# The 64-row parts of q, k and v of a token tile side by side, in the input products of a transformer block

## The chip, the core and the metric

The kernel runs on one core of a Trainium2 chip. A core has a matrix engine (TensorE, "PE" in the profile; "PEld" is its loading of the stationary operand), three elementwise engines (VectorE "DVE", ScalarE "ACT", GpSimd "POOL"), an engine that mostly issues transfers (SyncE "SP"), and DMA engines. Each engine works through its own list of instructions in order; semaphores tie the lists together. The metric is the device time of one execution in microseconds (us), the median of three runs.

## The reference

One block of a diffusion transformer over x of 2 batches x 2048 tokens x 576 features, 16 heads of 36, in float32:

```python
xn = _ln(x, 1e-06) * (1 + sc_msa) + sh_msa            # modulated from cond
qkv = (xn @ w_qkv + b_qkv).reshape(B, N, 3, H, hd)    # 576 -> 1728
q, k, v = qkv[:, :, 0], qkv[:, :, 1], qkv[:, :, 2]
q = _ln(q, 1e-05, qn_g, qn_b)                         # per head
k = _ln(k, 1e-05, kn_g, kn_b)
attn = softmax(einsum('bqhd,bkhd->bhqk', q, k) * hd ** (-0.5))
o = einsum('bhqk,bkhd->bqhd', attn, v).reshape(B, N, C)
x = x + g_msa * (o @ w_proj + b_proj)
xn2 = _ln(x, 1e-06) * (1 + sc_mlp) + sh_mlp
x = x + g_mlp * (gelu(xn2 @ w1 + b1) @ w2 + b2)
```

## The kernel before

The work goes in stages: a short preparation of the conditioning, then for each batch the input stage (norm, q/k/v products), attention, and the output product; then the two products of the MLP for both batches. The change touches the input stage only, which is the function `inputs` (line 868).

**Tiling of the input products.** A batch is 16 token tiles of 128 tokens. The 576 features are the contracted dimension: four full chunks of 128 and one of 64. A product (q, k or v of one token tile) has two halves of 288 columns, which lie in two banks of one PSUM tile. Each half needs four matmuls over 128 rows (`whole`, line 376, matmuls on line 379) and one over 64 rows (`halved`, line 387, matmuls on line 390). The two 64-row matmuls of a product use the upper and the lower half of TensorE's rows: half 0 reads rows 0 to 63, half 1 rows 64 to 127 of a chunk that is stored twice. Going from 128-row to 64-row matmuls changes how TensorE's array is divided into tiles.

`two_products` (line 394) orders the two parts of a product by a running number 3t + w: even ones do `whole` then `halved`, odd ones `halved` then `whole`. So the 64-row parts of two products in a row lie side by side, four matmuls in a group, and there are 24 such groups in the 48 products of a batch.

**What else happens in a token tile.** Around the products stand, for each tile t:
- `next_rows` (941): the rows of tile t+2 are loaded and normed on VectorE (lines 272 to 279), with a root and a copy on ScalarE;
- `input_by_feature` (851): the normed rows of tile t+1 are transposed on TensorE (lines 357, 358) into a PSUM tile, and five ScalarE activations (line 365) apply the modulation and write `xnt`, the stationary operand of the next tile's products;
- bias additions on VectorE, which empty the PSUM tile of a product: line 960 for q and k into `both`, line 967 for v into the value tile `vt`;
- `centred` (877): head means of `both` are taken off on VectorE (lines 883 to 885), and ScalarE squares the rest (890);
- `head_scale` (892) for tile t-1: sums of squares (895), a root on ScalarE (901), a reciprocal (903), and the product on GpSimd (905);
- `by_feature` (910) for tile t-2: nine transposes of q and k on TensorE (915) into two PSUM tiles, which VectorE (924) and ScalarE (920) empty with gain and bias. At some tiles it also prepares keys or queries for attention on VectorE (lines 792, 793) whose DMAs were issued a call before.

**What sets the order.** TensorE's list follows the program's text throughout, VectorE's follows it within `inputs`; the lists of ScalarE, GpSimd and SyncE are ordered by a scheduler. PSUM tiles of this stage come from a pool of four (two banks each, `s_tile`, line 86); a fifth waits for the oldest to be emptied. Attention that follows takes all eight banks singly (`bank`). The last tile of a batch centres q and k one by one and does its own `head_scale` at once, so that attention can transpose the last two tiles between its first scores (`last`, line 935). Attention's first steps are `scores` (line 1012), exponentials on ScalarE (line 1016), and `values` (line 1025).

Of the kernel before, what the change touches and what calls it, by code (L numbers as in the profile page):

```python
# [12 lines left out]
ALU = mybir.AluOpType  # L13
# [9 lines left out]
FULL = 4  # L23
# [8 lines left out]
def dit_block(  # L32
# [25 lines left out]
    nc = tc.nc  # L58
    B, N, C = x.shape
    MLP = w1.shape[1]  # L60
    HD = qn_g.shape[0]
    H = C // HD
    NT = N // P
    NPAIR = H // 2
    HALF = C // 2
# [20 lines left out]
    def s_tile():  # L86
        return psum["s"].tile([P, 2, 512], F32, tag="s", name="s")
# [35 lines left out]
    def halves(ap):  # L123
        return ap.rearrange("p (a f) -> p a f", a=2)
# [15 lines left out]
    with tc.tile_pool(name="bound", bufs=1, side="right") as bound:  # L140
# [11 lines left out]
        product = bound.tile([1, 1], F32, name="product")  # L152
# [223 lines left out]
    def whole(outs, stationary, moving, first):  # L376
        for a in range(2):
            for k in range(FULL):
                nc.tensor.matmul(  # L379
                    outs[a],  # L380
                    stationary(k, a),
                    moving(k, a),
                    start=(first and k == 0),
                    stop=(not first and k == FULL - 1),
                )

    def halved(outs, stationary, moving, first):
        for a in range(2):
            r = slice(64 * a, 64 * a + 64)
            nc.tensor.matmul(  # L390
                outs[a], stationary(FULL, a)[r], moving(FULL, a)[r], start=first, stop=not first
            )

    def two_products(outs, stationary, moving, turn):


        parts = (whole, halved) if turn % 2 == 0 else (halved, whole)
        for part in parts:
            part(outs, stationary, moving, part is parts[0])
# [325 lines left out]
    def block_of_small():  # L725
# [16 lines left out]
        vv = vt[:, 0 : NT * H * HV].rearrange("p (t h e) -> p t h e", t=NT, h=H)  # L742
# [108 lines left out]
        def input_by_feature(b, rows):  # L851
            xnt = xs["pool"].tile([P, NKC, P], F32, name="xnt", bufs=2)
            modulated(xnt, rows, 0, b)
            return xnt
# [13 lines left out]
        def inputs(b, weights, work, xnt, loaded):  # L868

            wq, wq4, bq = weights  # L870
            normed, squares, taken = {}, {}, []
            key_tiles = (0, 4, 8, 12, 14, 16)

            def banks_of_two():
                return [bank for ps in (s_tile(), s_tile()) for bank in (ps[:, 0], ps[:, 1])]

            def centred(both, w0=0, w1=2):

                part = both[:, w0 * C : w1 * C]
                heads = part.rearrange("p (h d) -> p h d", d=HD)  # L880
                n = (w1 - w0) * H
                sums = work.tile([P, 2 * H], F32, name="sums", bufs=2)
                nc.vector.tensor_reduce(sums[:, :n], heads, AX.X, ALU.add)
                nc.vector.tensor_scalar_mul(sums[:, :n], sums[:, :n], 1.0 / HD)
                nc.vector.tensor_tensor(
                    heads, heads, sums[:, :n].unsqueeze(2).to_broadcast([P, n, HD]), ALU.subtract
                )
                if w0 == 0:
                    squares["sq"] = work.tile([P, 2 * C], F32, name="sq")
                nc.scalar.activation(squares["sq"][:, w0 * C : w1 * C], part, AF.Square)  # L890

            def head_scale(t, both, parts=((0, 2),)):
                var = work.tile([P, 2 * H], F32, name="var")
                for w0, w1 in parts:
                    nc.vector.tensor_reduce(
                        var[:, w0 * H : w1 * H],
                        squares["sq"][:, w0 * C : w1 * C].rearrange("p (h d) -> p h d", d=HD),
                        AX.X,
                        ALU.add,
                    )  # L900
                nc.scalar.activation(var, var, AF.Sqrt, bias=eps5, scale=1.0 / HD)
                inv = work.tile([P, 2 * H], F32, name="inv")
                nc.vector.reciprocal(inv, var)
                heads = both.rearrange("p (h d) -> p h d", d=HD)
                nc.gpsimd.tensor_tensor(
                    heads, heads, inv.unsqueeze(2).to_broadcast([P, 2 * H, HD]), ALU.mult
                )
                normed[t] = both

            def by_feature(t, banks, chunks=range(NQK), all_on_vector=False):  # L910
                both, begun = normed[t], [*taken]
                taken.clear()
                parts = [(c, banks[i // 4][:, i % 4 * P : i % 4 * P + P]) for i, c in enumerate(chunks)]
                for c, ps in parts:
                    nc.tensor.transpose(ps, both[:, c * P : (c + 1) * P], ident)  # L915

                for c, ps in parts[::-1]:
                    dst = chunk(c, slice(t * P, (t + 1) * P))
                    if c < 4 and not all_on_vector:
                        nc.scalar.activation(  # L920
                            dst, ps, AF.Identity, bias=bias_qk[:, c : c + 1], scale=gain_qk[:, c : c + 1]
                        )
                    else:
                        nc.vector.tensor_scalar(
                            dst, ps, gain_qk[:, c : c + 1], bias_qk[:, c : c + 1], ALU.mult, ALU.add
                        )
                for do in begun:
                    do()
                if t == TPB - 1:
                    taken.append(take_q(0, 0))  # L930
                if t + 1 in key_tiles and NQK - 1 in chunks:
                    i = key_tiles.index(t + 1)
                    taken.append(take_k_block(*key_tiles[i - 1 : i + 1]))

            def last(t, chunks):
                by_feature(t, [bank() for _ in range(0, len(chunks), 4)], chunks, True)
                left = [*taken]
                taken.clear()
                return left

            def next_rows(t):
                return tile_normed(loaded.pop(0)) if loaded else input_rows(b, t, nc.sync)

            rows = next_rows(1)
            before = None
            for t in range(NT):
                both = work.tile([P, 2 * C], F32, name="both", bufs=3)
                for w in range(3):
                    ps = s_tile()
                    two_products(  # L950
                        [ps[:, a, :HALF] for a in range(2)],
                        lambda k, a: xnt[:, k, :],
                        lambda k, a: (
                            wq[:, k, w * C + a * HALF : w * C + (a + 1) * HALF] if k < FULL else wq4[:, w, :]
                        ),
                        3 * t + w,
                    )
                    bias = halves(bq[:, w * C : (w + 1) * C])
                    if w < 2:
                        nc.vector.tensor_tensor(  # L960
                            halves(both[:, w * C : (w + 1) * C]), ps[:, :, :HALF], bias, ALU.add
                        )
                        if w == 0 and t > 0:
                            head_scale(t - 1, before)
                    else:
                        heads = "p a (h d) -> p a h d"
                        nc.vector.tensor_tensor(
                            vv[:, t, :, 0:HD].rearrange("p (a h) d -> p a h d", a=2),
                            ps[:, :, :HALF].rearrange(heads, d=HD),
                            bias.rearrange(heads, d=HD),  # L970
                            ALU.add,
                        )

                    if w == (1 if t % 2 == 0 else 0):
                        if t + 1 < NT:
                            ahead = input_by_feature(b, rows)
                        if t >= 2:
                            by_feature(t - 2, banks_of_two())
                        if t + 2 < NT:
                            rows = next_rows(t + 2)  # L980

                    if t == NT - 1 and w < 2:
                        centred(both, w, w + 1)
                    if t == NT - 1 and w == 1:
                        head_scale(t, both, ((0, 1), (1, 2)))
                if t + 1 < NT:
                    centred(both)
                before, xnt = both, ahead

            return last  # L990
# [624 lines left out]
```

## Time and profile before

| | |
|---|---|
| three runs | 3227.92, 3229.68, 3230.13 us; median 3229.68 |
| profiled execution | 3230.55 us, of it a span of 3228.7 us |
| TensorE busy | 3205.6 us (99% of the span) |
| VectorE, ScalarE, GpSimd busy | 1451.2, 1496.8, 355.1 us |
| input stage of the second batch (from 1118.0 to 1359.3 us) | TensorE 241.3, VectorE 158.3, ScalarE 79.3, GpSimd 32.4 us busy |
| share of the chain that ended last: line 379, line 390 | 16%, 2% |

The span is the profiled part from the first to the last instruction of the core; the execution's own time is a little longer. A line of a group names the source line, the engine, the operation, what is written and what is read, the shapes, how often, then busy time in us, the mean duration of one in ns, and the engine's idle time before them with what ended it. Each float32 matmul shows as two records of TensorE. Records of matmuls overlap, since they are pipelined, so distances between starts are the better measure of TensorE's time. Line 379 serves the input products and the output product, which the names of the tiles tell apart (`wq,xnt` and `wp,qo`). A line of the timeline gives start, duration and what ran, with consecutive equal instructions merged.

### The profile page before, as it was taken

Reading aid. Unit: us, or ns where it says so; the run is one execution under the profiler, and the core shown is the slowest. Engines: PE = TensorE matmul, PEld = TensorE weight load, DVE = VectorE, ACT = ScalarE, POOL = GpSimd, SP = SyncE. Lnnn points to the kernel's source line nnn. Section 1 sums busy time; section 2 is a strip of 40 time slices with the busy share of each in tenths; the row PEclk is TensorE's granted clock in tenths of the full one; section 3 lists DMA queues with packets and bytes.
Section 4 is the critical chain, followed back from the end, with each engine's and each line's share of the span. In section 5 each row is a group of like instructions: output and inputs, shape, how many; then the busy total and the mean of one; then the engine's idle time right before and its main releaser. Section 6 shows DMA issues by size and latency. Waiting matters only on the chain.

```text
span 3228.7 us, 46968 instructions
## 1 busy us (share of the span) xinstructions
PE 3205.6 (99%) x18143; PEld 1883.0 (58%) x18143; DVE 1451.2 (45%) x2131; ACT 1496.8 (46%) x2952; POOL 355.1 (11%) x432
## 2 busy tenths in 40 slices
PE   8999999999999999999999999999999999999999
PEld 5775333333333777733333333358888888777777
DVE  4674333333333366633333333345555544455454
ACT  2335666666666033366666666633555552000000
POOL 1111000112110111100001111010000000111111
PEclk9999999999999999999999999999999999999999
DMA  3112212223231400122222223154322223433331
GB/s 131 26 26 65 76 35 68 66 70 83 69 85 34 146 26 24 27 56 46 50 44 65 68 66 74 47 173 156 120 90 88 93 80 110 153 132 111 118 103 38
DMA packets 129332, 253.16 MB, mean 78 GB/s; under 512 B 22979, under 2 KB 68492, under 8 KB 127052
## 3 DMA queue, kind: packets, MB, share of 16 engines
q1 hardware_dynamic: 105588, 182.07, 18.5%
q0 software_dynamic: 22640, 66.23, 7.4%
q8 instruction: 145, 2.38, 0.3%
q10 hardware_dynamic: 872, 1.77, 0.2%
q14 instruction: 87, 0.71, 0.1%
HBM read 135.40 MB, written 66.35 MB: 62 GB/s over the span
## 4 chain that ended last, share of the span: by engine, by line
PE 99%; DMA 1%; SPq 0%; DVE 0%; issue 0%; DVEq 0%
PE b L1025 28%; PE b L1012 19%; PE s L379 16%; PE s L1527 15%; PE m L1368 12%; PE s L390 2%; PE m L1382 2%; PE one L1368 2%; PE s L915 1%; PE s L357 1%; PE t L1428 0%; DMA wq<-in_w_qkv_dram 0%; DMA wa<-in_w_ada_dram 0%; PE b L192 0%; PE b L915 0%; DMA km<-qo 0%
## 5 line engine op out<-in xcount | busy, mean ns | idle before, releaser
L1016 ACT ACTIVATE pt<-b 128x512 f32<-128x512 f32 x2048 | 1057.4, 608 | 485.6 <-PE b L1025 270.8
L1025 PE MATMUL b<-pt,vt 128*64 128x512 f32 x4096 | 935.0, 598 | 0.0
L1025 PEld LDWEIGHTS b<-pt,vt 128*64 128x64 f32 x4096 | 271.9, 136 | 582.0 <-issue 438.8
L1012 PE MATMUL b<-qm,km 32*128 32x512 f32 x4096 | 566.5, 614 | 0.2 <-DMA km<-qo 0.2
L1073 DVE TENSOR_TENSOR ot<-b,ot 128x512 f32<-128x512 f32 x192 | 132.8, 691 | 653.2 <-PE b L1025 652.7
L1012 PE MATMUL b<-qe,ke 16*128 16x512 f32 x2048 | 422.8, 790 | 0.0
L379 PE MATMUL s<-wq,xnt 128*128 128x288 f32 x1536 | 392.9, 411 | 3.9 <-DMA wq<-in_w_qkv_dram 3.2
L1527 PE MATMUL s<-ws,as 128*128 128x288 f32 x1440 | 351.8, 406 | 0.0
L1012 PEld LDWEIGHTS b<-qm,km 32*128 32x128 f32 x4096 | 191.6, 184 | 269.3 <-ACT pt L1016 205.0
L379 PEld LDWEIGHTS s<-wq,xnt 128*128 128x128 f32 x1536 | 286.4, 191 | 95.5 <-issue 18.9
L1527 PEld LDWEIGHTS s<-ws,as 128*128 128x128 f32 x1440 | 273.6, 190 | 75.6
L1044 DVE RECIPROCAL den<-den 128x512 f32<-128x512 f32 x64 | 213.6, 3337 | 12.3 <-DMA den<-den_dram 12.3
L1368 PE MATMUL m<-xnt,wb 128*128 128x256 f32 x864 | 213.8, 383 | 0.0
L1368 PE MATMUL m<-s,wb 128*128 128x256 f32 x864 | 210.1, 379 | 0.2 <-DVE s L1338 0.2
L1071 DVE COPY ot<-b 128x512 f32<-128x512 f32 x64 | 44.3, 692 | 334.7 <-PE b L1025 334.7
L1368 PEld LDWEIGHTS m<-xnt,wb 128*128 128x128 f32 x864 | 159.1, 190 | 32.2 <-issue 11.9
L1368 PEld LDWEIGHTS m<-s,wb 128*128 128x128 f32 x864 | 164.1, 190 | 22.9 <-DVE s L1338 0.6
L1012 PEld LDWEIGHTS b<-qe,ke 16*128 16x128 f32 x2048 | 108.1, 184 | 114.4 <-issue 113.0
L1395 DVE TENSOR_TENSOR cs<-m,cs 128x512 f32<-128x512 f32 x72 | 49.7, 690 | 213.1 <-ACT cs L1394 151.7
L1527 PE MATMUL s<-ws,hidden 128*128 128x288 f32 x576 | 142.3, 406 | 0.0
L1505 DVE TENSOR_TENSOR as<-hidden 128x1152 f32<-128x1152 f32 x80 | 139.0, 1801 | 0.0
L365 ACT ACTIVATE xnt<-s,mod 128x128 f32<-128x128 f32 x180 | 66.8, 460 | 152.7 <-PE s L358 152.7
(174 smaller groups left out, 2553.5 us busy)
## 6 DMA issues: line engine op xcount, KB each, us to landing
gelu<-cs SPq DMA_DIRECT2D x144, 256.0 KB
hidden<-gelu SPq DMA_DIRECT2D x16, 2304.0 KB
den<-den_dram SPq DMA_DIRECT2D x128, 128.0 KB
x_dram<-kr POOLq DMA_DIRECT2D x48, 288.0 KB, 2.8
qm<-qo SPq DMA_DIRECT2D x192, 64.0 KB
kr<-in_x_dram POOLq DMA_DIRECT2D x32, 288.0 KB, 3.8
xr<-x_dram SPq DMA_DIRECT2D x32, 288.0 KB
out_dram<-y POOLq DMA_DIRECT2D x30, 288.0 KB, 3.8
```

Of the source, the lines that this page charges most:

```text
L365: nc.scalar.activation(dst[:, k, :], t4[:, k * P : (k + 1) * P] if k < FULL else t1[:, :P], AF.Identity, bias=mod[:, which, k, b : b + 1], ...
L379: nc.tensor.matmul(outs[a], stationary(k, a), moving(k, a), start=(first and k == 0), stop=(not first and k == FULL - 1),)
L390: nc.tensor.matmul(outs[a], stationary(FULL, a)[r], moving(FULL, a)[r], start=first, stop=not first)
L1012: nc.tensor.matmul(ps, k[r, keys], q[r, :], start=first, stop=not first)
L1016: nc.scalar.activation(pt[:, h, :], banks[2 * c + h], AF.Exp, scale=SCALE)
L1025: nc.tensor.matmul(acc[64 * h : 64 * h + 64, :], vt[:, v0 : v0 + 64], pt[:, h, :], start=pt is pts[0][0], stop=pt is pts[-1][0],)
L1044: nc.vector.reciprocal(den, den)
L1073: nc.vector.tensor_tensor(ot, acc, ot, ALU.add)
L1368: nc.tensor.matmul(out_m[m], wb[:, slot[m], k, f * P : (f + 1) * P], moving[m](k), start=k == 0 and (m == 1 or (first and m in (2, 5, 6))) ...
L1382: nc.tensor.matmul(out_m[m], w[r, f * P : (f + 1) * P], a[r, FULL, t * PAIR : (t + 1) * PAIR], start=first and m != 4, stop=not first and ...
L1505: nc.vector.tensor_tensor(stationary[m], x_, y_, op)
L1527: nc.tensor.matmul(ms[m], stationary[m][:, f, :], ws[m][:, f, :], start=(f == 0), stop=(f == HF - 1))
```

## The change

The three products of a token tile are no longer made one after the other. Each gets its PSUM tile from `product`, and its two parts are issued apart: the full-row part of q, then the transposes of the next tile's rows and the norm of the rows after, the full-row part of k, then the 64-row parts of q, k and v side by side, six matmuls in one group, and then the full-row part of v. The 64-row part of v is the first of its sum, those of q and k are the last of theirs. The bias additions follow as `biased`, and `by_feature` of tile t-2 stands at the end of the tile instead of after q or k. The last tile (`final`) has no next tile: it puts the 64-row parts of q and k together, and makes v on its own at the end, with its 64-row part last; there the bias addition of v comes before the last `head_scale`.

```diff
+            def product(w, xnt):
+                ps = s_tile()
+                return ps, (
+                    [ps[:, a, :HALF] for a in range(2)],
+                    lambda k, a: xnt[:, k, :],
+                    lambda k, a: (
+                        wq[:, k, w * C + a * HALF : w * C + (a + 1) * HALF] if k < FULL else wq4[:, w, :]
+                    ),
+                )
+
+            def biased(w, ps, t, both):
+                bias = halves(bq[:, w * C : (w + 1) * C])
+                if w < 2:
+                    nc.vector.tensor_tensor(halves(both[:, w * C : (w + 1) * C]), ps[:, :, :HALF], bias, ALU.add)
+                else:
...
             for t in range(NT):
                 both = work.tile([P, 2 * C], F32, name="both", bufs=3)
-                for w in range(3):
-                    ps = s_tile()
-                    two_products(
...
-                        3 * t + w,
-                    )
...
-                        if w == 0 and t > 0:
-                            head_scale(t - 1, before)
...
-                    if w == (1 if t % 2 == 0 else 0):
-                        if t + 1 < NT:
-                            ahead = input_by_feature(b, rows)
-                        if t >= 2:
-                            by_feature(t - 2, banks_of_two())
-                        if t + 2 < NT:
-                            rows = next_rows(t + 2)
-
-                    if t == NT - 1 and w < 2:
-                        centred(both, w, w + 1)
-                    if t == NT - 1 and w == 1:
-                        head_scale(t, both, ((0, 1), (1, 2)))
-                if t + 1 < NT:
+                final = t == NT - 1
+                q, q_parts = product(0, xnt)
+                whole(*q_parts, True)
+                if not final:
+                    ahead = input_by_feature(b, rows)
+                    if t + 2 < NT:
+                        rows = next_rows(t + 2)
+                k, k_parts = product(1, xnt)
+                if not final:
+                    whole(*k_parts, True)
+                    v, v_parts = product(2, xnt)
+                halved(*q_parts, False)
+                halved(*k_parts, final)
+                if not final:
+                    halved(*v_parts, True)
+                biased(0, q, t, both)
+                if t > 0 and final:
+                    head_scale(t - 1, before)
+                if final:
+                    whole(*k_parts, False)
+                    centred(both, 0, 1)
+                    biased(1, k, t, both)
+                    by_feature(t - 2, banks_of_two())
+                    v, v_parts = product(2, xnt)
+                    whole(*v_parts, True)
+                    halved(*v_parts, False)
+                    centred(both, 1, 2)
+                    biased(2, v, t, both)
+                    head_scale(t, both, ((0, 1), (1, 2)))
+                else:
+                    biased(1, k, t, both)
+                    if t > 0:
+                        head_scale(t - 1, before)
+                    whole(*v_parts, False)
+                    biased(2, v, t, both)
+                    if t >= 2:
+                        by_feature(t - 2, banks_of_two())
                     centred(both)
                 before, xnt = both, ahead
```

More of the change, by code (lines that the diff above doesn't have):

```diff
@@ L942, in next_rows @@
                 return tile_normed(loaded.pop(0)) if loaded else input_rows(b, t, nc.sync)
+            def product(w, xnt):
[12 more added lines that the diff above has]
+                else:
+                    heads = "p a (h d) -> p a h d"
+                    nc.vector.tensor_tensor(
+                        vv[:, t, :, 0:HD].rearrange("p (a h) d -> p a h d", a=2),
+                        ps[:, :, :HALF].rearrange(heads, d=HD),
+                        bias.rearrange(heads, d=HD),
+                        ALU.add,
+                    )
             rows = next_rows(1)
@@ L947, in inputs @@
                 both = work.tile([P, 2 * C], F32, name="both", bufs=3)
-                for w in range(3):
-                    ps = s_tile()
-                    two_products(
[L951 to L955, printed above, removed]
-                        3 * t + w,
-                    )
[L958 to L962, printed above, removed]
-                        if w == 0 and t > 0:
-                            head_scale(t - 1, before)
[L965 to L972, printed above, removed]
-                    if w == (1 if t % 2 == 0 else 0):
-                        if t + 1 < NT:
-                            ahead = input_by_feature(b, rows)
-                        if t >= 2:
-                            by_feature(t - 2, banks_of_two())
-                        if t + 2 < NT:
-                            rows = next_rows(t + 2)
-                    if t == NT - 1 and w < 2:
-                        centred(both, w, w + 1)
-                    if t == NT - 1 and w == 1:
-                        head_scale(t, both, ((0, 1), (1, 2)))
```

## The prediction

> **What bounds the kernel now.** I read the page's engine shares and its chain first, then the groups of the two product lines, then the chain in order of time, and last the timeline around the end of the input stage of the second batch. The share of the chain by engine:
>
> ```profile
> PE 99%; DMA 1%; SPq 0%; DVE 0%; issue 0%; DVEq 0%
> ```
>
> TensorE is the whole chain, so only its own time counts, plus any wait that the change gives it. The groups of the two product lines (busy us, mean ns, idle before):
>
> ```profile
> L379 PE MATMUL s<-wq,xnt 128*128 128x288 f32 x1536 | 392.9, 411 | 3.9 <-DMA wq<-in_w_qkv_dram 3.2
> L390 PE MATMUL s<-wq,xnt 64*128 64x288 f32 x384 | 59.6, 429 | 0.0
> ```
>
> Each matmul of the program is two records ("passes"): 768 full-row and 192 half-row ones. They wait only at the very start. From the chain in time, 32 passes of the output stage with no 64-row part between:
>
> ```profile
> 2160.78 7.76 PE s L379 x32
> ```
>
> So a pass costs 7.76/32 = 0.2425 us. From the timeline, the last tiles of the second batch (start, duration, engine, line):
>
> ```profile
> 1343.93 1.24 PE L390 MATMUL s<-wq,xnt 64*128 64x288 f32 x8
> 1345.10 4.15 PE L379 MATMUL s<-wq,xnt 128*128 128x288 f32 x16
> ...
> 1349.09 1.15 PE L915 MATMUL s<-ident,both 128*128 128x128 f32 x9
> ...
> 1350.07 4.05 PE L379 MATMUL s<-wq,xnt 128*128 128x288 f32 x16
> ...
> 1352.03 1.27 DVE L924 TENSOR_SCALAR kr<-s,gb_qk 128x128 f32<-128x128 f32 x4
> ...
> 1353.53 0.74 DVE L883 TENSOR_REDUCE sums<-both 128x16 f32<-128x576 f32 x1
> ...
> 1354.04 1.24 PE L390 MATMUL s<-wq,xnt 64*128 64x288 f32 x8
> ...
> 1355.19 0.75 DVE L960 TENSOR_TENSOR both<-s,bq 128x576 f32<-128x576 f32 x1
> 1355.21 4.15 PE L379 MATMUL s<-wq,xnt 128*128 128x288 f32 x16
> ...
> 1357.65 1.58 DVE L895 TENSOR_REDUCE var<-sq 128x16 f32<-128x576 f32 x2
> ...
> 1359.27 0.32 ACT L901 ACTIVATE var<-var,eps 128x32 f32<-128x32 f32 x1 [0.82 <-DVE var L895]
> 1359.29 1.14 PE L1012 MATMUL b<-qm,km 32*128 32x512 f32 x8
> 1359.61 1.28 ACT L1016 ACT_TABLE_LOAD   x1
> ...
> 1359.96 0.69 DVE L967 TENSOR_TENSOR vt<-s,bq 128x576 f32<-128x576 f32 x1
> ...
> 1360.90 4.03 ACT L1016 ACTIVATE pt<-b 128x512 f32<-128x512 f32 x8
> ...
> 1366.38 3.65 PE L1025 MATMUL b<-pt,vt 128*64 128x512 f32 x16
> ```
>
> Two things are to be seen. Eight half-row passes run in pairs: 1354.04 to 1355.21 is 1.17 us, where four slots are 0.97. Full-row blocks beside them are long too: 3.97 (1350.07 to 1354.04) and 3.99 (1345.10 to 1349.09) against 16 x 0.2425 = 3.88. One change there and back costs 0.09 + 0.20 + 0.11 = 0.40 us. And at the hand-over to attention TensorE starts scores at 1359.29, but ScalarE can start the exponentials only after the root of the last head_scale (1359.27) and a table load, at 1360.90; the first value matmul follows at 1366.38, 7.09 after the scores' start.
>
> [...] L967 runs at 1359.96 behind the last head_scale, though TensorE had gone on to scores at 1359.29. [...] here L379 idles 3.16 us for weights before 28.28, and its next 16 passes take 5.63 instead of 3.88.
>
> **The change, part by part.** *Removed changes.* Before, a batch has 24 half-row groups (one per two products); after, 17 (one per tile, two in the last). First I test the count on the second batch of before: 768 passes 186.24, 96 slots 23.28, 24 round trips 9.60, 15 times five transposes 15 x 0.55, 14 times nine transposes 14 x 0.98, 0.09 into scores and one odd 0.17 at 1228.55: 241.35. Measured: 1117.97 to 1359.29, 241.32. So TensorE never waits there.
>
> After, a token tile without by_feature is 48 x 0.2425 + 0.55 + 6 x 0.2425 + 0.40 = 14.04 us, one with it 15.02; the last tile of the second batch starts 2 x 14.04 + 13 x 15.02 = 223.3 us after the first (taken as 223.37 unrounded). Seven fewer round trips are 2.8 us per batch.
>
> *Waits inside a tile.* A tile now holds four PSUM tiles at once, as many as there are. In order: q waits for k's bias addition of the tile before, the input transposes for v's, k for the ninth by_feature chunk's eviction, v for ScalarE's last by_feature eviction. On a clock that starts with q: v needs its bank at 9.1; VectorE finishes the five evictions at 1.9 and ScalarE its four 1.5 later, at 3.5, so 5.6 us are left. VectorE per tile: three additions 2.3, head_scale 2.1, evictions 1.7, centred 3.0, row norm 2.4: 11.5 of 15.0. Moved row norms (3 more in the first batch, some 6 us in tile 13) make its k addition end near 13.3, before q of the next tile at 15.0. With this cover the cost is nothing; without it, what is late is the next tile's first matmul. SP's order of DMAs is the same as before; two POOL DMA issues (1.1 us) move ahead of the last head_scale's product, and are done at 15.5, before its inputs (18).
>
> *Start of the first batch.* Weights of k arrive at 28.28. Before, q's and k's half-row passes (4 slots and a round trip) fill the wait; now they come after it, and the five transposes (0.55) go before. After: k whole 28.28 to 33.91 (cold clock as before), six slots with their trip to 35.66, v whole to 39.65 = start of tile 1; the last tile starts 14.04 + 13 x 15.02 later, at 248.98.
>
> *The last tile, clock from its q.* TensorE: half-rows at 3.97, k whole 5.14, by_feature 9.13, v whole 10.11, v's half-rows 14.08, done 14.67. VectorE, in its new order, by the distances of the timeline: evictions of tile 12 from 0.21, their part of k 1.93, centring of tile 14 from 3.20 to 6.16, q addition to 6.92, ScalarE's square to 7.42, head_scale of 14 (2.07) to 9.57, centring q (1353.53 to 1355.19: 1.66) to 11.23, k addition (0.79) to 12.02, evictions of tile 13 (1.50) to 13.52, centring k (1.67) to 15.19, v addition to 15.9, both reduces (1.62) to 17.52 = last root. Exponentials 1.63 later (1359.27 to 1360.90), at 19.15; first value matmul 5.48 later, at 24.63. That is 9.9 us after the scores could start, against 7.09: 2.8 us lost per batch, since v's addition now stands ahead of the last head_scale and v's product is itself the last thing TensorE makes. Even with an idle VectorE v's addition could not begin before 14.9, so the loss is at least 2.5. Behind the late root stand, on ScalarE, the table load and all exponentials; on TensorE, the transposes of tile 14, which need a bank that the first exponential frees.
>
> *Sum.* Second batch, first q to first value matmul: 223.37 + 24.63 = 248.00 against 1366.38 - 1117.97 = 248.41: -0.4. First batch: 248.98 + 24.63 = 273.61 against 273.20: +0.4. All later stages have their order unchanged. The sum is 0.0 on the profiled execution (3230.55 us, of it a span of 3228.7), which lies 0.9 above the median; I predict the median, 3229.7.
>
> **The rivals.** (1) The gain arrives whole, because the hand-over isn't lengthened: -0.4 - 2.8 and +0.4 - 2.8, 3224.1; for it: ScalarE and VectorE are idle a third or more of the stage; against: their order and strict queues. If the early transposes also keep the clock up at 28.28, 1.8 us more: 3222.3. (2) It ends slower: PSUM. With all four tiles in use, one late release stalls TensorE in every tile: ScalarE's by_feature evictions, queued behind row statistics and squares, free v's bank. It decides from 0.25 us per tile (6.5 us over the 26 tiles that follow evictions), which needs them 5.9 us later than I have; at 0.4 us it gives 3240.1. For it: before, no wait had to hold in each tile alike; against: the slack. (3) The hand-over is dearer: VectorE another 1 us late in both batches and a half-clock window: +2 to +5, 3233. (4) The change doesn't regroup the passes: excluded by the instruction order, where six half-row matmuls stand side by side.
>
> **How the numbers follow.** Mine 0.66, (1) 0.12, (2) 0.08, (3) 0.14. A measurement of this kernel can tell about 0.2% (6.5 us) from no change. Within it lie mine, (3) mostly, and (1) without the clock: same 0.86; slower 0.10 ((2) and the end of (3)); faster 0.04. Mine alone spans 3227.5 to 3232.5 (0.5 us per hand-over, 2 us of clock); 8 in 10 reaches from (1) nearly whole to (3): 3225 to 3235.
>
> **What would show it.** Right: 34 half-row groups instead of 48; tiles 15.0 us apart with no idle TensorE; last root near 17.5 and exponentials near 19.2 after the last tile's q; value matmuls 9.9 after v's half-rows end. Wrong: L379 or L390 with releasers ACT L920 or DVE in the middle of the stage; exponentials near 16.5; 16 fast passes after 28.28.

## The result, and the profile after

The changed kernel takes 3235.87 us (median of 20 runs, 3233.75 to 3241.67); the kernel before, beside it, 3229.50 us (20 runs, 3227.92 to 3230.45). The ratio is 1.0022, with a 95% interval of 1.0015 to 1.0029. So the change costs about 6.4 us, where the prediction was 3229.7 us with a range up to 3235. The profiled execution of the changed kernel took 3235.14 us, 4.59 more than that of before; its span is 3233.3 us.

The page's share of the chain by engine, in the changed kernel:

```profile
PE 97%; DVE 1%; DMA 1%; ACT 0%; SPq 0%; issue 0%; DVEq 0%; ACTq 0%
```

TensorE was 99% of the chain before and VectorE 0%; VectorE, with 1%, is new in it. The two groups of the input products in the changed kernel (busy us, mean ns, idle before them and what ended it):

```profile
L379 PE MATMUL s<-wq,xnt 128*128 128x288 f32 x1536 | 392.8, 410 | 3.8 <-DMA wq<-in_w_qkv_dram 3.0 <-ACT xnt L859 0.8
L390 PE MATMUL s<-wq,xnt 64*128 64x288 f32 x384 | 55.8, 421 | 0.0
```

As many matmuls as before, 3.8 us less busy time in the half-row ones, and no wait beyond that of the very start: inside the tiles nothing was lost. The loss is at the end of the input stage, at the hand-over to attention: the way from the last products over the scores and exponentials to the first value matmul. The timeline of the last tile of the second batch in the changed kernel (start, duration, engine, line), with the same lines of work that the prediction showed of before:

```profile
1343.81 4.05 PE L379 MATMUL s<-wq,xnt 128*128 128x288 f32 x16
...
1353.35 0.69 DVE L883 TENSOR_REDUCE sums<-both 128x16 f32<-128x576 f32 x1
1353.58 2.13 POOL L905 TENSOR_TENSOR both<-both,inv 128x1152 f32<-128x1152 f32 x1 [9.83 <-PE s L915]
...
1354.08 1.66 DVE L884 TENSOR_SCALAR sums<-sums 128x16 f32<-128x16 f32 x1
1355.77 0.76 DVE L885 TENSOR_TENSOR both<-both,sums 128x576 f32<-128x576 f32 x1
...
1357.90 0.76 PE L390 MATMUL s<-wq,xnt 64*128 64x288 f32 x4
...
1360.37 0.75 DVE L961 TENSOR_TENSOR vt<-s,bq 128x576 f32<-128x576 f32 x1
...
1362.47 0.32 ACT L901 ACTIVATE var<-var,eps 128x32 f32<-128x32 f32 x1 [1.30 <-DVE var L895]
...
1364.11 4.03 ACT L1041 ACTIVATE pt<-b 128x512 f32<-128x512 f32 x8
...
1371.00 0.64 PE L1050 MATMUL b<-pt,vt 128*64 128x512 f32 x1
```

TensorE's last half-rows start 14.09 us after the tile's first q matmul, as reckoned. But the last root comes 18.66 after it, the exponentials 20.30, and the first value matmul 27.19. Two things are to be seen. Line 884 is a tensor_scalar over 16 numbers per partition; it takes 1.66 us, and ends 0.03 us after GpSimd's product of line 905 (1353.58 + 2.13 = 1355.71). And from the first exponential to the first value matmul it is 6.89 us, where it was 5.48 before.

The second is TensorE's clock. The profile records what share of it was granted, and in these traces that is either 1.00 or 0.50; a stretch at 0.50 is called a half-clock window here. Busy time by stretch in the changed kernel (the stretch; its length; the busy time and number of instructions of TensorE, its weight load, VectorE, ScalarE and GpSimd; then the granted clock, DMA share and GB/s):

```profile
28.70:32.11 3.41, 3.41 (x8) 2.37 (x8) 0.00 (x0) 0.00 (x0) 0.00 (x0) 0.50 0.97 355
...
271.05:274.46 3.41, 3.41 (x20) 3.29 (x20) 1.76 (x5) 2.20 (x5) 0.15 (x1) 0.50 0.40 68
1361.50:1366.70 5.20, 3.83 (x28) 2.21 (x22) 2.37 (x7) 4.20 (x8) 3.21 (x3) 1.00 0.31 70
1366.73:1370.14 3.41, 3.41 (x21) 3.24 (x19) 1.42 (x4) 2.22 (x5) 0.00 (x0) 0.50 0.35 54
```

In the 5.20 us before 1366.70 TensorE is busy for 3.83 only: eight banks of scores are full, and it waits for the exponentials to free one (1.22 us idle before 1364.85, ended by line 1041). Then its clock is 0.50 for 3.41 us, just when the scores that the first value matmuls stand behind are made. The first batch has such a window too (271.05 to 274.46). In the profiled execution of before such windows lie only behind the wait for k's weights at the start (28.22 to 31.63 us) and at the program's very end (from 3226.51).

Stage by stage the difference of the two profiled executions adds up: the first batch's first value matmul is 2.29 us later than before, the second batch's stretch from first q to first value matmul is 250.62 us against 248.41, 2.21 more, and the stages after either are equal within 0.15 (844.8 us before and 844.9 after; 765.7 and 1096.6 in both). Together 4.5 of the 4.59.

### The profile page after: what moved, and what is told of

Same layout as the page of the kernel before. It is cut to its first block, busy times and chain, and to the rows that moved or that the text cites. A ratio compares the mean times of both kernels' runs of the same rounds, so it can differ in the third digit from the quotient of the medians.

```text
span 3233.3 us, 46997 instructions
## 1 busy us (share of the span) xinstructions
PE 3205.5 (99%) x18143; PEld 1889.1 (58%) x18143; DVE 1455.6 (45%) x2131; ACT 1494.9 (46%) x2952; POOL 352.7 (11%) x432
## 4 chain that ended last, share of the span: by engine, by line
PE 97%; DVE 1%; DMA 1%; ACT 0%; SPq 0%; issue 0%; DVEq 0%; ACTq 0%
PE b L1050 28%; PE b L1037 19%; PE s L1552 15%; PE s L379 15%; PE m L1393 12%; PE m L1407 2%; PE s L390 2%; PE one L1393 2%; PE s L915 1%; PE s L357 0%; PE t L1453 0%; DMA wq<-in_w_qkv_dram 0%; DMA wa<-in_w_ada_dram 0%; DMA km<-qo 0%; PE b L192 0%; DVE kr L924 0%
## 5 line engine op out<-in xcount | busy, mean ns | idle before, releaser
L1431 ACT ACTIVATE cs<-cs,b_sb 128x512 f32<-128x512 f32 x144 | 98.8, 719 | 68.2 <-DVE cs L1426 31.4
```

Of the source, the lines that this page charges most:

```text
L1431: nc.scalar.activation(part, part, AF.Gelu, bias=b1_sb[:, g : g + 1])
```

## The experiments

After this profile the theory has two causes: (a) VectorE's chain to the last root is longer than reckoned, because of line 884; (b) TensorE's half-clock windows at the two hand-overs to attention. The rivals: it is one cause seen twice, or the regrouped tiles themselves cost something. Each ratio is to runs of before on the same chip at the same time; before's median there was between 3228.7 and 3229.5, which is how far times of different comparisons can be set side by side.

**The last two tiles as before.** All tiles but the last two keep the new order; the last two are made by the old loop, which leaves 17 half-row groups in a batch.

```diff
             for t in range(NT):
                 both = work.tile([P, 2 * C], F32, name="both", bufs=3)
+                if t >= NT - 2:
+                    for w in range(3):
...
+                    before, xnt = both, ahead
+                    continue
                 final = t == NT - 1
```

> The last two token tiles of each batch are made as before the change, the other fourteen as after it; 17 half-row groups per batch, as in the changed kernel. My theory, that all of the loss is made between the last products and the first value matmul: first q to first value matmul is 3.1 us shorter than before in the second batch and 2.3 us shorter in the first, the hand-over is 7.1 us from scores to value matmul as before, one half-clock window less per batch, and the time is 5.4 us under before: 3224.1 (ratio 0.9983). The rival, that the loss belongs to the token tiles themselves or to later stages: 3231 or more, over before.

Measured: 3226.56 us (3225.37 to 3229.16, 21 runs), ratio to before 0.9993 (0.9986 to 0.9999). Most of the loss is gone, and the kernel is faster than before, but by less than the regrouped tiles should give. There is no half-clock window at either hand-over, and exponential to value matmul is 5.47 and 5.48 us again. The rest shows in the timeline of the second batch:

```profile
1354.95 1.12 PE L1080 MATMUL b<-qm,km 32*128 32x512 f32 x2
...
1355.62 0.69 DVE L992 TENSOR_TENSOR vt<-s,bq 128x576 f32<-128x576 f32 x1
...
1356.37 0.77 PE L1080 MATMUL b<-qm,km 32*128 32x512 f32 x3 [0.30 <-DVE vt L992]
...
1357.65 4.03 ACT L1084 ACTIVATE pt<-b 128x512 f32<-128x512 f32 x8 [1.10 <-PE b L1080]
```

After the first score matmul (two records) TensorE stands until v's bias addition is done, and the exponentials are 2.70 us behind the first score (1.61 before). In this kernel v's PSUM tile lies in banks that attention's first scores take (in before, and in the changed kernel, in banks that they take later): the regrouping of the earlier tiles changed which banks were free for it. So this run has a wait of its own, which a later one shortens.

**q centred ahead of GpSimd's product.** In the last tile q is centred between the sums and the reciprocal of tile 14's `head_scale`; GpSimd's product, which needs the reciprocal, starts after it.

```diff
-                    head_scale(t - 1, before)
+                    head_scale(t - 1, before, between=lambda: centred(both, 0, 1))
...
-                    centred(both, 0, 1)
```

> The changed kernel with one move in the last token tile: q is centred on VectorE between the sums of squares of the tile before and their reciprocal, so that GpSimd's product of that tile starts after it and not during it. My theory, that the small tensor_scalar of q's centring (1.66 us instead of 0.17) stands still because GpSimd works at that moment: it takes 0.17 again, the last root comes about 1.5 us sooner in each batch (17.2 us after the tile's first q matmul instead of 18.7), the first exponential too, and the time is 3 us under the changed kernel, about 3233. The rival, that the 1.66 us belong to the operation's own operands or its wait: it stays near 1.6 us and nothing moves by more than 0.3 us.

Measured: 3233.39 us (3227.38 to 3235.26, 21 runs), ratio 1.0011 (1.0005 to 1.0018). The group of line 884's small form, first in the changed kernel and then in this one (busy us, mean ns):

```profile
L884 DVE TENSOR_SCALAR sums<-sums 128x16 f32<-128x16 f32 x4 | 3.7, 914 | 0.1
```

```profile
L884 DVE TENSOR_SCALAR sums<-sums 128x16 f32<-128x16 f32 x4 | 0.7, 175 | 0.1
```

3.0 us over the two batches were the cost of running beside GpSimd's product. The last root of the second batch comes 17.00 us after the tile's first q matmul, where 17.2 was expected and the changed kernel has 18.66. It is not the engine as a whole that is held: in this run line 925's evictions, which read PSUM, start at 1353.68, inside GpSimd's product (1353.30 to 1355.43), and take their usual 1.35 us for four. Both half-clock windows stayed in the profiled run (exponential to value matmul 6.91 and 7.12 us). The runs of this kernel fall mostly in two groups by the mean clock granted in them: six at 0.999 have a median of 3229.5 us, twelve at 0.997 one of 3234.4. So the same program gets more half-clock time in some executions than in others, and some 5 us go with it. The profiled run is one of the six, the slowest (3232.2); the twelve must have had further windows beside its two, and where those lay is not shown.

**Work for TensorE across the hand-over.** The changed kernel, with the second four groups of scores of each batch's first step made three times over, each time from the start, so that nothing is left out.

```diff
+                    again = 3 if (p, qb, g) == (0, 0, 0) and k0 == (2 * g + 1) * P else 1
-                    for k, q, first in (
+                    for k, q, first in again * (
```

> The changed kernel with the second four groups of scores of each batch's first step computed three times (the same result, 16 more score matmuls per batch), in the gap in which TensorE waits for the first exponential. My theory, that TensorE's half-clock window after the wait costs 1.3 to 1.4 us per batch: the window at 1366.7 us (and that at 271 us) is gone, exponential to value matmul is 5.5 us again instead of 6.7 to 6.9, the extra matmuls are hidden but for 0.4 us, and the time is about 2 us under the changed kernel, 3234, with less spread between runs. The rival, that the slow matmuls there are a matter of waits for ScalarE and the clock decides nothing: no gain, or 0.5 to 1 us slower for the added work.

Measured: 3233.18 us (3229.19 to 3235.97, 21 runs), ratio 1.0014 (1.0007 to 1.0021). The second batch of the profiled run:

```profile
1354.27 1.12 PE L1038 MATMUL b<-qm,km 32*128 32x512 f32 x2
...
1359.79 4.03 ACT L1042 ACTIVATE pt<-b 128x512 f32<-128x512 f32 x8
...
1365.27 3.65 PE L1051 MATMUL b<-pt,vt 128*64 128x512 f32 x16
```

Both windows are gone, and exponential to value matmul is 5.46 and 5.48 us, although TensorE makes 16 more score matmuls in each batch; the exponentials are as late as in the changed kernel (5.52 us after the first score). So (b) is a cost of its own, which more work takes away. This execution is the fastest of the 21, and one execution could have missed the windows by chance; but the mean clock speaks for all of them: 0.998 or 0.999 in every run here, 0.996 to 0.998 in every run of the changed kernel. The spread of the times shrank little (6.8 us against 7.9).

**Both at once.** The two diffs above together.

> Both single corrections at once: q centred ahead of GpSimd's product, and the second four groups of scores of each batch's first step computed three times, so that TensorE has work across the hand-over. Each alone took some 2.5 us off the changed kernel's 3235.9. Theory (two terms that add up): 3230.7, between 3229.5 and 3231.5. Rival (one cause seen twice): 3233, as each alone.

Measured: 3227.36 us (3226.65 to 3230.78, 13 runs), ratio 0.9996 (0.9988 to 1.0004). This is better than either theory had it. The second batch of the profiled run:

```profile
1355.28 0.32 ACT L901 ACTIVATE var<-var,eps 128x32 f32<-128x32 f32 x1 [1.68 <-DVE var L895]
...
1356.92 4.03 ACT L1042 ACTIVATE pt<-b 128x512 f32<-128x512 f32 x8
...
1362.40 1.08 PE L1051 MATMUL b<-pt,vt 128*64 128x512 f32 x4
```

The last tile's first q matmul is at 1338.28; the root follows at 17.00, the exponential at 18.64, the value matmul at 24.12. The prediction had 17.52, 19.15 and 24.63. With both causes away the hand-over is as it was reckoned, a little better. In the profiled runs the two add up: from first q to first value matmul of the second batch the corrections took 1.43 and 1.42 us off the changed kernel's 250.62, both together 3.07. The medians add up to more (2.5 and 2.7 alone, 8.5 together); the runs of the single corrections still vary in the clock they were granted, those of this one hardly (11 of 13 at 0.999). That fits, but one execution of each kernel was profiled, so where the windows of the others lay is open.

**More changes of tiling.** In 15 tiles of a batch q's half-rows follow q's full rows again: 15 more groups.

```diff
                 whole(*q_parts, True)
                 if not final:
+                    halved(*q_parts, False)
                     ahead = input_by_feature(b, rows)
...
-                halved(*q_parts, False)
+                if final:
+                    halved(*q_parts, False)
                 halved(*k_parts, final)
```

> The changed kernel with q's two half-row matmuls moved back behind q's full-row part, in fifteen of the sixteen token tiles: one more change of tiling there and back in each of these tiles and nothing else. My theory, that a change there and back costs 0.40 us of TensorE and that TensorE sets the time of these tiles: 15 x 2 x 0.40 = 12.0 us over the changed kernel, 3248 (ratio to before 1.0057), tiles 15.42 us apart instead of 15.02. The rival, that the change of tiling is partly hidden behind transposes or stationary loads: 3 to 8 us.

Measured: 3243.24 us (3239.76 to 3244.53, 5 runs), ratio 1.0045 (1.0031 to 1.0058), 7.4 more than the changed kernel. The second batch takes 243.47 us from first q to first score against 238.20: 5.27 us for 15 round trips, 0.35 each. The whole is less than the 12.0 expected, and lies in the range of the rival that had part of the price hidden; the profiled executions, 4.6 us apart, show how that comes about. In this one the half-clock windows lay ahead of the exponentials, where TensorE waits anyway (267.88 and 1366.97; exponential to value matmul 5.47 and 5.48 us); there was none behind k's weights, where the changed kernel's 16 records took 1.7 us longer; k's weights came 0.6 us earlier; and one extra group falls into the wait for them. The price per trip is confirmed, 0.05 smaller than the 0.40 of the sum; the rival that the regrouping is worth nothing in the tiles is out.

**The old last two tiles, v's addition earlier.** As the first experiment, with v's bias addition of the last tile between the last sums and the reciprocal.

```diff
+                        elif t == NT - 1:
+                            head_scale(t, both, ((0, 1), (1, 2)), between=lambda: biased(2, ps, t, both))
...
-                        if t == NT - 1 and w == 1:
-                            head_scale(t, both, ((0, 1), (1, 2)))
```

> The last two token tiles of each batch as before (their half-row groups change the tiling as before), and in the very last one v's bias addition stands between VectorE's last reductions and its reciprocal. In the run with the last two tiles as before, the first scores of each batch waited 1.1 and 1.4 us for that addition, because v's PSUM tile lay in banks that the scores take first. Theory (the change's gain in the tiles is whole, and all its loss is in the hand-over): scores to first exponential back to about 1.6 us in the second batch, some 2.5 us less than the 3226.6 of that run, so about 3224.1, five below before. Rival (the regrouped tiles cost something elsewhere too): the wait goes and the time stays at 3226.6.

Measured: 3224.94 us (3223.3 to 3228.6, 21 runs), ratio 0.9988 (0.9982 to 0.9995). Its hand-over in the second batch:

```profile
1351.46 1.69 PE L1075 MATMUL b<-qm,km 32*128 32x512 f32 x5
1351.57 0.76 DVE L962 TENSOR_TENSOR vt<-s,bq 128x576 f32<-128x576 f32 x1 [0.16 <-PE s L379]
...
1353.65 4.03 ACT L1079 ACTIVATE pt<-b 128x512 f32<-128x512 f32 x8 [0.59 <-PE b L1075]
```

The exponentials are 2.2 us behind the first score instead of 2.70, still not 1.6, since TensorE still reaches v's bank before the addition is over. The gain of the regrouped tiles comes through: 3.8 us below before, of the five expected.

**A new order of the last two tiles.** The changed kernel with q centred first, v's addition between the last sums and the reciprocal, and in the last tile but one the `by_feature` of tile 12 ahead of v's full rows.

```diff
-                    head_scale(t - 1, before)
+                    head_scale(t - 1, before, between=lambda: centred(both, 0, 1))
...
-                    centred(both, 0, 1)
...
-                    biased(2, v, t, both)
-                    head_scale(t, both, ((0, 1), (1, 2)))
+                    head_scale(t, both, ((0, 1), (1, 2)), between=lambda: biased(2, v, t, both))
...
+                    if t == NT - 2:
+                        by_feature(t - 2, banks_of_two())
                     whole(*v_parts, False)
...
-                    if t >= 2:
+                    if 2 <= t < NT - 2:
```

> The changed kernel with VectorE's and TensorE's work of the last two tiles put in another order: q's centring ahead of GpSimd's product, v's bias addition between the last reductions and the reciprocal, and the transposes of the third tile from the end ahead of v's full rows in the last tile but one. Theory (the loss is VectorE's chain to the last root, and then TensorE's half clock): first exponential 16.6 to 17.0 us after the last tile's first q matmul (20.3 in the changed kernel, 19.15 before), and 3225.5 in all; 3228 if the half-clock windows stay at both hand-overs. Rival (the hand-over is set by something else): above 3231.

Measured: 3225.34 us (3223.22 to 3226.82, 21 runs), ratio 0.9988 (0.9982 to 0.9995). In the second batch:

```profile
1353.47 0.32 ACT L901 ACTIVATE var<-var,eps 128x32 f32<-128x32 f32 x1 [0.82 <-DVE var L895]
...
1355.35 4.03 ACT L1042 ACTIVATE pt<-b 128x512 f32<-128x512 f32 x8 [0.26 <-PE b L1038]
...
1360.82 3.65 PE L1051 MATMUL b<-pt,vt 128*64 128x512 f32 x16
```

The tile's first q matmul is at 1338.28 (16 records of 0.2425 us after the 1334.40 at which v's full rows before it begin): root at 15.19, exponential at 17.07 (16.6 to 17.0 expected), value matmul at 22.54, and full clock at both hand-overs. From the first q to the first score the batch takes 238.15 us, against 241.32 before. All 17 groups are there, and no work is repeated: the loss was the order of VectorE's list and the half clock behind TensorE's pause, and nothing of the regrouping itself.

**The start, twice.** The changed kernel again, and beside it the changed kernel with the half-rows of q, k and v of the very first tile ahead of k's full rows.

```diff
+                opening = b == 0 and t == 0
...
                 if not final:
-                    whole(*k_parts, True)
+                    if not opening:
+                        whole(*k_parts, True)
...
-                halved(*k_parts, final)
+                halved(*k_parts, final or opening)
...
                 else:
+                    if opening:
+                        whole(*k_parts, False)
                     biased(1, k, t, both)
```

> The changed kernel once more, beside the next one. The hand-overs lose 4.5 us against the prediction's sum in the profiled run, the median of the changed kernel is 6.4 us above before's. If the rest is the start of the first batch (k's weights land between 26.4 and 29.4 us, and the clock may then be halved for 3.4 us, which costs 1.7), it comes and goes: 3233.5 to 3236 and again a spread of 6 us or more.

> The changed kernel, with only the first tile of the first batch in another order: the half-row parts of q, k and v ahead of k's full rows, in the wait for k's weights. If only the passes leave the path, 1.9 us below the changed kernel beside it; if they also keep TensorE's clock up at the start, up to 3.6 us below it and a smaller spread. The hand-overs stay as in the changed kernel: first exponential 20.3 us after the last tile's first q matmul in the second batch.

Measured: the changed kernel 3238.01 us (3233.6 to 3241.28, 6 runs), ratio 1.0030 (1.0018 to 1.0042); with the new first tile 3232.85 us (3231.12 to 3235.99, 21 runs), ratio 1.0013 (1.0007 to 1.0020). From the first matmul with k's weights to the first value matmul the profiled runs have 247.21 and 244.24 us. Of these 2.97 us, 1.86 are the passes that left the path and about 1.6 the half-clock window at the start, which this run of the changed kernel had and the other not; 0.5 went the other way at the hand-over (exponential to value matmul 6.70 us against 6.22). The last tile's times are unchanged (exponential 20.3 after the first q matmul). Both medians miss what was expected: the changed kernel came above its 3233.5 to 3236, 2 us higher than in its first set of runs, and the two lie 5.2 us apart instead of 1.9 to 3.6. The mean clock is low in both (0.996 or 0.997 in all 6 runs of the one and in 15 of 21 of the other); what makes the rest of the difference is not shown.

**The best version.** The old last two tiles with v's addition earlier, and the new first tile: the three diffs for these above.

> As the run before it in this list, and in the first tile of the first batch the half-row parts of q, k and v stand ahead of k's full rows, in the 3.0 us that TensorE waits there for k's weights: 6 passes of 0.2425 us and one change of tiling there and back of 0.40 us leave the path, 1.86 us. Theory: 1.9 us below the kernel it is built on, about 3222.2. Rival: k's weights land later or TensorE's clock at the start is lowered for longer, and nothing is won: the same as the kernel it is built on.

Measured: 3222.92 us (3221.71 to 3226.34, 21 runs), ratio 0.9981 (0.9974 to 0.9988): faster than both kernels, by 5.8 and some 13 us. The start, in this kernel's timeline:

```profile
23.79 1.73 PE L390 MATMUL s<-wq,xnt 64*128 64x288 f32 x12
...
26.73 11.91 PE L379 MATMUL s<-wq,xnt 128*128 128x288 f32 x48 [1.21 <-DMA wq<-in_w_qkv_dram]
```

The twelve half-row records end within the wait for k's weights, and the 48 full-row ones behind it run at some 0.245 us each from the first: the clock is not halved there in this execution. From k's weights to the first value matmul it is 240.00 us, against 241.83 without this edit: 1.83, where 1.86 was expected. The medians differ by 2.0.

## Why the prediction was wrong

Its mechanism held: fewer round trips in the tiles, paid back at the hand-over to attention. Its sum was 0.0; the profiled execution says +4.59. Step by step:

*Inside the tiles: right.* The price of a pass, the 17 groups, a tile of 15.02 us. The last q of the second batch came 223.43 us after the first (223.37 predicted), and no product line waits in the middle of the stage. The rival of the PSUM release is out by that.

*Start of the first batch: right, with luck.* k's weights came at 27.71 instead of 28.28, the clock was halved there as before, and the last tile started at 248.47 instead of 248.98. The halved clock was luck: of the eight profiled executions that open in this way, two have the half-clock window behind k's weights, two have it earlier, and four have none.

*The last tile's clock: wrong in two terms.* In us after its first q matmul, second batch:

| step of the sum | predicted | measured |
|---|---|---|
| v's half-rows start | 14.08 | 14.09 |
| head_scale of tile 14 done | 9.57 | 9.54 |
| q centred | 11.23 | 12.64 |
| k's addition done | 12.02 | 13.31 |
| evictions of tile 13 done | 13.52 | 14.90 |
| k centred | 15.19 | 16.56 |
| last root | 17.52 | 18.66 |
| first exponential | 19.15 | 20.30 |
| first value matmul | 24.63 | 27.19 |

The step that failed first is "centring q (1353.53 to 1355.19: 1.66)"; it took 3.10 (1353.35 to 1356.45). The time came from a place of the trace of before where GpSimd's product of the same `head_scale` was all but over when the tensor_scalar in the middle of the centring began:

```profile
1352.26 2.13 POOL L905 TENSOR_TENSOR both<-both,inv 128x1152 f32<-128x1152 f32 x1 [13.06 <-PE s L379]
...
1354.31 0.17 DVE L884 TENSOR_SCALAR sums<-sums 128x16 f32<-128x16 f32 x1
```

In the new order the tensor_scalar begins 0.50 us after the product does, and took 1.66 us instead of 0.17. VectorE's list then stays late by 1.4 us, 1.15 at the root. The run with q centred first shows that it is the company of the product: ahead of it the same instruction takes 0.17 us again. In the changed kernel it ends 0.03 us after the product; what holds it until then, no trace says. The prediction had priced the two engines as independent.

The second is "first value matmul 5.48 later". It was 6.89, and 6.73 in the first batch: the distance was taken from before, at full clock, and carried into a hand-over where TensorE pauses longer and its clock halves. Shown by the run with repeated scores, and by all traces together: of the 24 hand-overs in the twelve profiled executions, the eight with half clock for 3.4 us or more between exponential and value matmul take 6.22 to 7.12 us for this stretch, the sixteen others, with at most 0.4 us of it, 5.46 to 5.48. This was in rival (3), with a later VectorE besides; but there the window was one among several mishaps, at a chance of 0.14, and "+2 to +5" had only "a half-clock window" in it, not one in each batch.

The corrected sum: second batch 1.15 + 1.41 + 0.06 = 2.62, first batch 1.14 + 1.26 - 0.51 = 1.89 above the prediction's own, 4.5 in all, against the 4.59 measured. The prediction of the sum was for the profiled execution; the two medians lie 6.4 apart, 1.8 more. Most runs of the changed kernel were granted less clock (11 of 20 at a mean of 0.997, 4 at 0.996) than the profiled one (0.998), and in them the time is longer: 3236.0 and 3238.0 against 3235.1 in the median. A thousandth of clock over the whole time is 3.2 us, two such windows. So the rest is most likely one more window in a usual run than in the profiled one; where it lies is not shown. The second profiled execution of the changed kernel does have one more, two in a row at the first hand-over (266.01 to 272.84), but lost less there (6.22 us from exponential to value matmul, against 6.73).

*The range.* Its upper end allowed for one surprise at the hand-over. Two came at once, both in the place where TensorE has to wait for VectorE's list, which had no slack; the range should have gone to that sum.

## What to carry to other kernels

A duration holds for its neighbours: before a step is moved beside work of another engine, look in the trace for how long it takes beside that work: VectorE's tensor_scalar took 1.66 us beside GpSimd's product and 0.17 ahead of it. A saving on the bounding engine is worth its sum only up to the next place where that engine has to wait; price that hand-over line by line, and put the order of the waiting engine's list right in the same edit. A pause of TensorE can cost twice: the pause itself, and, where half clock followed as here, up to 1.7 us in the work just behind it (7.12 us from exponential to value matmul against 5.46).

## What the runs showed of the hardware

- A tensor_scalar of 16 numbers per partition, SBUF to SBUF, took 1.66 us beside a 2.13 us GpSimd product and 0.17 without. VectorE's evictions from PSUM beside the same product, with q centred first, were not slowed (four in 1.35 us).
- TensorE's half clock came in windows of 3.41 us (28.70 to 32.11, 271.05 to 274.46 and 1366.73 to 1370.14 in the changed kernel). The last of these followed a stretch of 5.20 us in which TensorE was busy for 3.83, not an idle one. The three starts lie 242.35 and 1095.68 us apart, 71 and 321 times 3.413.
- The length of a pause did not decide: pauses of 2.96 and 2.97 us before k's weights were followed by half clock in the two executions of the changed kernel, pauses of 2.94, 2.96 and 2.98 were not with q centred first, with repeated scores and in the new order. Nor did TensorE's busy time just before: in the changed kernel it was busy for 2.04 of the 3.41 us before 1366.73, and half clock followed; it was busy for 1.32 of the 3.10 us from 262.90, and the clock stayed at 1.00 until 271.05. What decides is not shown.
- The regrouping of earlier tiles decided in which PSUM banks the last v lay, and so how early attention's scores had to wait for its addition: in the first experiment the first score of the first batch waited (1.4 us), and the second score of the second batch (1.1 us).
- k's weights came between 26.4 and 29.4 us after the span's start in the profiled runs: the start alone can move a run by up to 3 us (an estimate from these times).
